# Second experts of a two-attention kernel take token chunks in the order in which attention completes them

## The chip, the core and the metric

The kernel runs on one core of a Trainium2 chip. The metric is the device time of one execution in microseconds (us), as the median of three runs. Beside the runs there is one profiled execution, whose trace every duration below is read from.

## What is computed

A residual stream of 1024 tokens with 512 columns passes four layers. Each normalises its input and adds its output to the stream.

```python
x = x + attn_a(layernorm(x))     # 32 heads of 16 columns, 8 groups of keys and values
x = x + ffn(layernorm(x))        # experts, first time
x = x + attn_b(layernorm(x))     # 32 causal heads of 128 columns, weights as 4-bit integers with scales
x = x + ffn(layernorm(x))        # the same experts, second time

def ffn(x):                      # 8 experts of rank 16, two of them per token
    base   = x @ W_base.T + b_base
    rw, sel = top_k(x @ W_router.T, 2)
    w      = softmax of rw, scattered to the 8 experts
    h      = x @ A[e].T                       # 16 numbers per expert
    return base + 2 * sum over e of w[e] * h[e] @ B[e].T
```

The change concerns the last head of attention b and the second use of the experts.

## The kernel before

**Names.** The stream lies in `x_sb`, four chunks `a` of 256 tokens, each with two halves `h` of 128 tokens. Tile `t` is half `t % 2` of chunk `t // 2`. `xT` holds the normalised stream with columns on partitions. `shared` holds the first experts' weights, and later `yT`, the sum over heads of attention b's output, with columns on partitions. `x_hl` holds the input of attention b split into two parts; after the last projection it takes the experts' weights again.

**Attention b.** For each of 32 heads `n` a loop runs over eight query tiles `t` in the order `TURNS = [0, 6, 1, 7, 2, 4, 3, 5]`. `probabilities` makes the scores (L846), the causal mask (L849), the largest score (L851, VectorE), the exponentials (L855, ScalarE), their sum and the division (L856, L857, VectorE), and moves the result with a DMA from `x_sb` to a `moved` buffer (L860). The stream is out of the way during attention b: it was stored in the DRAM tensor `x_kept` (L941), and the four chunks of `x_sb` serve as slots for probabilities, by the count of tiles modulo 4 (L852). Three tiles later (`LAG = 3`), `behind` turns the probabilities on TensorE (`transposed`, L878, copied by ScalarE at L879).

**Sets.** A head's tiles form two sets of chunks, `SETS = (0, 3), (1, 2)`. When all four tiles of a set are turned, `context` multiplies them with the values (L888), splits the result into a high part (L900, ScalarE) and a low part (L901, VectorE), and queues `project_out`. That multiplies with the output weights (L782, L783, four pairs of matmuls) and adds to `yT` on VectorE (L923, four instructions). Set 0 of a head is full after tiles 0, 6, 1, 7; set 1 after tiles 2, 4, 3, 5.

**What sets the order.** TensorE's order is the order of the calls in the source, interleaved by two lists: `short` and `long`. `fill` takes a share from a list, `complete` takes one named item to its end, `drain` takes both lists to their end. The orders of the other engines and of the DMA queue of SyncE (SP) are arranged when the program is built; each engine then works strictly in its order. PSUM banks for all of this come from one pool of five (`bank`).

**After the last head.** The source goes on as follows.

```python
while lagging:                       # three tiles left: 4, 3, 5
    behind(0); fill(short, shares[0]); behind(1); fill(long, shares[1])
nc.sync.dma_start(x_sb, x_kept)      # whole stream, one DMA of 2 MB
drain()
...
back(0); back(1); turned(0); back(2); moe.base(0); turned(1); back(3)
moe.route(0, 4); moe.base(1); turned(2); turned(3); moe.route(4, 8); ...
```

`back(a)` turns attention's output back (L1064, eight transposes on TensorE), adds it to the stream (L1065), takes the statistics (L154, L155), the scale (L159 to L161) and writes the normalised rows: half 0 on VectorE (L167), half 1 on ScalarE (L175). Then GpSimd adds the experts' bias to the stream (`bias`, L572). `turned(a)` turns the rows on TensorE (L190), copies them to `xT` alternately by ScalarE (L139) and VectorE (L141), and multiplies with the experts' first weights and the router (`hidden`, L579). `route(t0, t1)` picks two experts for four tiles with some twenty small VectorE instructions (L610 to L635). `base(t)` is the dense part (L591, four matmuls), `moe.turned` turns the weighted hidden numbers (L645), and `finish(t)` adds the experts' part (L652) and the stream (L654, VectorE). The result is stored by chunks (L1097, four DMAs of 512 KB).

Of the kernel before, what the change touches and what calls it, by code (L numbers as in the profile page):

```python
# [11 lines left out]
F32 = mybir.dt.float32  # L12
# [8 lines left out]
P = 128  # L21
S = 1024
C = 512
NC_ = C // P
NT = S // P
# [16 lines left out]
def kernel(  # L42
# [28 lines left out]
    nc = tc.nc  # L71

    def pool(stack, name, bufs=1, space=None):
        kw = {} if space is None else {"space": space}
        return stack.enter_context(tc.tile_pool(name=name, bufs=bufs, **kw))
# [5 lines left out]
    out_v = out.rearrange("(a p h) c -> p a h c", p=P, h=2)  # L81
    x_sb = const.tile([P, 4, 2, C], F32, name="x_sb")
    for a in range(4):
# [13 lines left out]
        fill=-BIG,  # L97
# [19 lines left out]
    AR = E * R + E  # L117
    fw = {}

    def place_ffn_weights(room):  # L120
        at = 0
        for name, n, width in ("base", NC_, C), ("ar", NC_, AR), ("b", 1, C), ("bias", 1, C):
            fw[name] = room[:, at : at + n * width].rearrange("p (c o) -> p c o", o=width)
            at += n * width
        return room[:, :at]
# [10 lines left out]
    def evacuate(dst, src):  # L136
        turn[0] += 1
        if turn[0] % 2:
            nc.scalar.copy(dst, src)  # L139
        else:  # L140
            nc.vector.tensor_copy(dst, src)  # L141

    class Norm:


        def __init__(self):
            self.st = const.tile([P, NT, 6], F32, name="st")
            self.mv = const.tile([P, NT, 2], F32, name="mv")
            self.rstd = const.tile([P, NT], F32, name="rstd")
            self.shift = const.tile([P, NT], F32, name="shift")  # L150
# [411 lines left out]
    class Experts:  # L562


        def __init__(self, name, sb, bank):
            self.name, self.sb, self.bank, self.ys = name, sb, bank, {}
            self.hl = sb.tile([P, NT, E * R + E], F32, name="hl")
            self.hw = sb.tile([P, NT, E, R], F32, name="hw")
            self.hwT = sb.tile([P, S], F32, name="hwT")
# [6 lines left out]
        def hidden(self, t):  # L576
            ph = self.bank()
            for c in range(NC_):
                nc.tensor.matmul(  # L579
                    ph[:, :AR],  # L580
                    xT[:, c, ts(t, P)],
                    fw["ar"][:, c, :],
                    start=(c == 0),
                    stop=(c == NC_ - 1),
                )
            evacuate(self.hl[:, t, :], ph[:, :AR])

        def base(self, t):
            py = self.ys[t] = self.bank()
# [59 lines left out]

        def finish(self, t):  # L650
            py = self.ys.pop(t)
            nc.tensor.matmul(py, self.hwT[:, ts(t, P)], fw["b"][:, 0, :], start=False, stop=True)  # L652
            a, h = t // 2, t % 2
            nc.vector.tensor_tensor(x_sb[:, a, h, :], x_sb[:, a, h, :], py, ALU.add)  # L654


    def attention_b():
# [5 lines left out]
        with ExitStack() as ph:  # L663
# [96 lines left out]
            def fill(lane, ns):  # L760
                credit[id(lane)] += ns
                while lane and credit[id(lane)] > 0:
                    credit[id(lane)] -= advance(lane, lane[0])
                if not lane:
                    credit[id(lane)] = 0

            def drain():
                while short or long:
                    fill(short, 4 * FAST)
                    fill(long, SLOW)  # L770

            def complete(name):
                for lane in (short, long):
                    for item in [q for q in lane if q[0] == name]:
                        while item in lane:
                            advance(lane, item)
# [61 lines left out]
            def probabilities(n, t):  # L838

                qT, kT = qTs[n], kTs[n // J]  # L840
                keys = (t + 1) * P
                wide = t >= NT // 2 or (n == 0 and t == 1)
                sc = sc_ps.tile([P, S if wide else C], F32, tag=f"sc{wide}", name="sc")
                for k0 in range(0, keys, C):
                    k1 = min(k0 + C, keys)
                    nc.tensor.matmul(  # L846
                        sc[:, k0:k1], qT[:, ts(t, P)], kT[:, k0:k1], start=True, stop=(k1 < keys)
                    )
                nc.tensor.matmul(sc[:, ts(t, P)], ident_bf, causal_bf, start=False, stop=True)  # L849
                m = work.tile([P, 1], F32, tag="m", name="m", bufs=3)  # L850
                nc.vector.tensor_reduce(m, sc[:, :keys], AX.X, ALU.max, negate=True)  # L851
                p = x_sb[:, len(issued) % 4].rearrange("p h c -> p (h c)")  # L852
                issued.append(t)
                total = work.tile([P, 1], F32, tag="total", name="total", bufs=3)
                nc.scalar.activation(p[:, :keys], sc[:, :keys], AF.Exp, bias=m, accum_out=total)  # L855
                nc.vector.reciprocal(total, total)  # L856
                nc.vector.tensor_scalar_mul(p[:, :keys], p[:, :keys], total)  # L857

                moved = late[0].tile([P, S if wide else C], F32R, tag=f"moved{wide}", name="moved")
                nc.sync.dma_start(moved[:, :keys].bitcast(F32), p[:, :keys])  # L860
                return moved
# [41 lines left out]
                short.append([("o", n, which), 8 * FAST, project_out(n, which)])  # L903

            HALVES = 4

            def project_out(n, which):

# [24 lines left out]
            with tc.manual_schedule(engines={mybir.EngineType.PE}):  # L933
# [62 lines left out]
                def behind(part):  # L996
                    n, t, p = lagging[0]
                    which = int(t // 2 in SETS[1])
                    if part == 0:
                        complete(("c", n - 1, which))  # L1000
                    if part == 0 or t >= 4:
                        transposed(n, t, p, 4 * part)
                    if part:
                        lagging.pop(0)
                        seen[n, which] = seen.get((n, which), 0) + 1
                        if seen[n, which] == 4:
                            complete(("v", n // J))
                            cost = 18 * P * SLOW // C
                            long.append([("c", n, which), cost, context(n, which)])

                for n in range(HEADS):
# [29 lines left out]
                    complete(("q", n + 1))  # L1041
                    if j == J - 1:
                        complete(("k", g + 1))
                while lagging:
                    behind(0)
                    fill(short, shares[0])
                    behind(1)
                    fill(long, shares[1])
                nc.sync.dma_start(x_sb, x_kept)
                drain()  # L1050
                late.pop()
                last.close()
                sb = pool(ph, "f2_sb")
                moe = Experts("2", sb, bank)
                xns = [sb.tile([P, 2, C], F32, name=f"xn{i}") for i in range(2)]
                weights = place_ffn_weights(x_hl.rearrange("p i c s -> p (i c s)").bitcast(F32))
                nc.sync.dma_start(weights, w_kept)

                def back(a):
                    for h in range(2):  # L1060
                        py = bank()
                        for c in range(NC_):
                            y = yT[:, c, ts(a, 2 * P)].rearrange("q (p h) -> q h p", h=2)
                            nc.tensor.transpose(py[:, ts(c, P)], y[:, h], ident)  # L1064
                        nc.vector.tensor_tensor(x_sb[:, a, h, :], x_sb[:, a, h, :], py, ALU.add)  # L1065
                    norm.stats(a)
                    norm.scale(a, a + 1)
                    norm.rows(a, xns[a % 2])
                    moe.bias(a)

                def turned(a):
                    norm.turned(a, xns[a % 2], bank, False, to_xT)
                    for t in (2 * a, 2 * a + 1):
                        moe.hidden(t)

                back(0)
                back(1)
                turned(0)
                back(2)
                moe.base(0)  # L1080
                turned(1)
                back(3)
                moe.route(0, 4)
                moe.base(1)
                turned(2)
                turned(3)
                moe.route(4, 8)
                moe.base(2)
                moe.turned(0, 4)
                for t in range(NT):  # L1090
                    moe.finish(t)
                    if t + 3 < NT:
                        moe.base(t + 3)
                    if t == 2:
                        moe.turned(4, 8)
                    if t % 2:
                        nc.sync.dma_start(out_v[:, t // 2], x_sb[:, t // 2])  # L1097

    attention_a()
    attention_b()  # L1100
# [69 lines left out]
```

## Time and profile before

| what | value |
| --- | --- |
| median of 3 runs | 1600.74 us (1598.55 to 1603.12) |
| the profiled execution's own time | 1601.31 us |
| its span, first to last instruction | 1599.5 us |
| TensorE (PE) busy | 1531.5 us, 96% of the span |
| VectorE (DVE) busy | 1241.1 us, 78% |
| ScalarE (ACT) busy | 783.0 us, 49% |
| GpSimd (POOL) busy | 482.6 us, 30% |
| mean granted TensorE clock | 0.987 of full speed |
| last score of the last head | 1512.5 us |
| start of the first `back` on TensorE | 1529.9 us |
| last matmul | 1595.1 us |

The page of the profile gives busy time by engine and, in 40 slices, where it lies. The timeline lists an engine's instructions in order, with the idle time in front of each in brackets and what ended it. The chain of waits follows the work that ended last backwards. The rows of windows give, for a stretch, the busy time of PE, PEld (weight load), DVE, ACT and POOL, then the granted clock, the share of the DMA engines and GB/s.

### The profile page before, as it was taken

To read this page: it belongs to the slowest core of one execution; us is meant where nothing else is said; L and a number is where in the kernel's file an instruction comes from. 1 tells how busy PE (TensorE), PEld (TensorE's weight loads), DVE (VectorE), ACT (ScalarE), POOL (GpSimd) and SP (SyncE) were. 2 spreads that over 40 slices of the span, in tenths; PEclk is the share of its full clock that TensorE was granted. 3 is DMA by queue.
4 is the path that set the end of the run, shared out by engine and by line. 5 is a ranking of instruction groups with operands and counts; after the bars stand their busy time and mean duration, and the time that the engine had idled before them with its cause. 6 is when DMAs were issued, how large, how long until landed. Compare 5 with 4: busy or idle time off the path is not lost.

```text
span 1599.5 us, 24080 instructions
## 1 busy us (share of the span) xinstructions
PE 1531.5 (96%) x8119; PEld 990.9 (62%) x8119; DVE 1241.1 (78%) x2290; ACT 783.0 (49%) x1694; POOL 482.6 (30%) x382
## 2 busy tenths in 40 slices
PE   7899999999999989999999999999999999999978
PEld 4244444444445457777777777777777777777764
DVE  4689888799755686788888878888788788788763
ACT  2067666576673245544544544444444444454420
POOL 5200000000103154436336336335435335333120
PEclk9899999999999989999999999999999999999999
DMA  5432322324304133333334334333333334333311
GB/s 126 81 81 47 54 49 48 66 36 88 91 3 110 66 105 125 108 139 124 116 131 139 112 119 135 116 119 126 120 120 121 109 120 129 105 112 129 140 50 53
DMA packets 98010, 158.63 MB, mean 99 GB/s; under 512 B 14320, under 2 KB 53936, under 8 KB 97504
## 3 DMA queue, kind: packets, MB, share of 16 engines
q1 hardware_dynamic: 97024, 155.46, 32.6%
q0 software_dynamic: 864, 1.64, 0.7%
q8 instruction: 65, 1.06, 0.3%
q14 instruction: 57, 0.47, 0.1%
HBM read 33.03 MB, written 6.05 MB: 24 GB/s over the span
## 4 chain that ended last, share of the span: by engine, by line
PE 80%; DVE 12%; ACT 3%; issue 2%; DMA 2%; SPq 1%; POOL 0%; ACTq 0%; DVEq 0%; POOLq 0%
PE pc L888 16%; PE sc L846 15%; PE po L413 7%; PE sc L339 6%; PE pp L782 5%; DVE m L348 5%; PE pp L783 5%; PE tp L878 5%; PE py L782 3%; PE py L783 3%; PE bank L591 3%; PE pp L273 2%; PE st L380 2%; PE py L453 2%; PE st L388 2%
## 5 line engine op out<-in xcount | busy, mean ns | idle before, releaser
L348 DVE TENSOR_REDUCE m<-sc 128x1 f32<-128x512 f32 x512 | 320.7, 681 | 37.3 <-PE st L380 21.7
L855 ACT ACTIVATE x_sb<-sc,m 128x768 f32<-128x768 f32 (+7 forms) x256 | 189.7, 741 | 317.1 <-DVE m L851 311.2
L392 ACT ACTIVATE pT<-st 128x512 f32<-128x512 f32 x512 | 264.7, 603 | 125.6 <-PE st L388 111.7
L846 PE MATMUL sc<-kT,qT 128*128 128x512 f32 (+3 forms) x768 | 293.1, 491 | 4.5 <-ACT x_sb L855 2.9
L851 DVE TENSOR_REDUCE m<-sc 128x1 f32<-128x768 f32 (+7 forms) x256 | 192.7, 753 | 132.5 <-PE sc L849 130.9
L888 PE MATMUL pc<-xT,v_sb 128*128 128x256 f32 (+1 forms) x1024 | 248.5, 373 | 5.0 <-DVE acc L796 2.5
L339 PE MATMUL sc<-ks,qs 64*128 64x512 f32 x512 | 187.0, 455 | 9.8 <-DMA ks<-k_hl 4.5
L857 DVE TENSOR_SCALAR x_sb<-x_sb,total 128x768 f32<-128x768 f32 (+7 forms) x256 | 190.0, 743 | 4.6 <-DVE total L856 0.3
L888 PEld LDWEIGHTS pc<-xT,v_sb 128*128 128x128 f32 x1024 | 176.0, 190 | 21.8 <-DVE acc L796 3.2
L846 PEld LDWEIGHTS sc<-kT,qT 128*128 128x128 f32 x768 | 139.6, 193 | 74.8 <-issue 63.8
L339 PEld LDWEIGHTS sc<-ks,qs 64*128 64x128 f32 x512 | 83.5, 186 | 158.5 <-DVE m L348 128.1
L380 PE MATMUL st<-qs,ks 64*128 64x512 f32 x512 | 177.4, 425 | 2.9 <-ACT pT L392 1.7
L388 PE MATMUL st<-ms_q,ones 64*128 64x512 f32 x512 | 179.0, 414 | 0.3 <-DMA ms_q<-mT 0.3
L923 DVE SCALAR_TENSOR_TENSOR shared<-py,o_sc,shared 128x512 f32<-128x512 f32 x248 | 176.1, 739 | 3.8 <-PE py L783 3.7
L808 POOL TENSOR_TENSOR qT<-acc,cos_sb 128x512 f32<-128x512 f32 x62 | 81.7, 1318 | 298.6 <-DVE total L856 203.1
L782 PE MATMUL pp<-x_hl,w 128*128 128x512 f32 x384 | 167.4, 436 | 1.9 <-DVE acc L796 1.3
L879 ACT COPY xT<-tp 128x512 f32<-128x512 f32 (+2 forms) x320 | 137.2, 471 | 63.9 <-PE tp L878 63.6
L783 PE MATMUL pp<-x_hl,w 128*128 128x512 f32 x384 | 152.7, 398 | 2.4 <-DVE x_hl L740 2.4
L690 POOL TENSOR_SCALAR w<-r 128x512 fp32r<-128x512 int32 x80 | 123.5, 1544 | 102.9 <-PE pp L783 69.8
L796 DVE SCALAR_TENSOR_TENSOR acc<-pp,q_sc,acc 128x512 f32<-128x512 f32 x192 | 142.9, 745 | 13.4 <-ACT acc L794 7.0
L878 PEld LDWEIGHTS tp<-ident_r,moved 128*128 128x128 f32 x1152 | 125.3, 141 | 37.0 <-issue 2.2
L413 PE MATMUL po<-pT,v_sb 128*32 128x512 f32 x1024 | 137.5, 608 | 0.0
(169 smaller groups left out, 2176.4 us busy)
## 6 DMA issues: line engine op xcount, KB each, us to landing
turned<-acc SPq DMA_DIRECT2D x160, 128.0 KB
moved<-x_sb SPq DMA_DIRECT2D x32, 512.0 KB
moved<-x_sb SPq DMA_DIRECT2D x32, 448.0 KB
moved<-x_sb SPq DMA_DIRECT2D x32, 384.0 KB
moved<-x_sb SPq DMA_DIRECT2D x32, 320.0 KB
qs<-shared SPq DMA_DIRECT2D x128, 64.0 KB
r<-in_qwq_dram SPq DMA_DIRECT2D x32, 256.0 KB
r<-in_qwo_dram SPq DMA_DIRECT2D x32, 256.0 KB
```

Of the source, the lines that this page charges most:

```text
L339: nc.tensor.matmul(sc, qs[pair % NS][rows, jj, ts(t, P)], ks[pair // 2 % NS][rows, ts(half, C)], start=True, stop=True,)
L348: nc.vector.tensor_reduce(ms[pair][:, at : at + 1], sc, AX.X, ALU.max, negate=True)
L380: nc.tensor.matmul(st, ks[pair // 2 % NS][rows, ts(kt, P)], qs[pair % NS][rows, u // 2, ts(u % 2, C)], start=True, stop=False,)
L388: nc.tensor.matmul(st, ones[rows], ms_q[pair % 2][rows, u // 2, ts(u % 2, C)], start=False, stop=True)
L392: nc.scalar.activation(pTs[pair, kt][:, u], st, AF.Exp, scale=DA**-0.5)
L413: nc.tensor.matmul(po[ts(u, 32), :], v_sb[:, kt, pair // 2, :], pT[:, u], start=(kt == 0), stop=(kt == NT - 1),)
L782: nc.tensor.matmul(ps, lhsT, high, start=True, stop=False)
L783: nc.tensor.matmul(ps, lhsT, low, start=False, stop=True)
L846: nc.tensor.matmul(sc[:, k0:k1], qT[:, ts(t, P)], kT[:, k0:k1], start=True, stop=(k1 < keys))
L851: nc.vector.tensor_reduce(m, sc[:, :keys], AX.X, ALU.max, negate=True)
L878: nc.tensor.transpose(tp[:, k - k0, :].bitcast(F32R), p[:, ts(k, P)], ident_r)
L888: nc.tensor.matmul(pc[:, 2 * P * i + lo : 2 * P * (i + 1)], v_sb[:, k, ts(g, DB)], place[pair][:, k, lo:], start=(k == 0), stop=(k == 2 * ...
```

## The change

1. In the last head, the slot of a tile's probabilities is taken from `SLOTS = 0, 1, 2, 3, 0, 3, 1, 2`: tile 4 goes to slot 3 (before: 1), tile 3 to slot 1 (before: 2), tile 5 to slot 2 (before: 3).
2. The stream comes back by chunks, in four DMAs of 512 KB, chunks 0 and 3 ahead of the last three tiles' turning in the source, chunks 1 and 2 behind it.
3. After the last head's loop, `project_out` of the head before and the last head's first context (chunks 0 and 3) are taken to their end; the first `project_out` follows after the turning of tile 4, `back(0)` after that of tile 3, and `back(3)` after that of tile 5.
4. The normalised rows of all four chunks have a place of their own, in columns 0 to 511 of `v_sb` (values of groups 0 to 3); before, two buffers were used in turn.
5. The second experts take the chunks in the order 0, 3, 1, 2, and tiles in the order 0, 1, 6, 7, 2, 3, 4, 5. Routing, `base` and `finish` follow that order; the biases are added after all four `back`.
6. The result is stored by tiles, in eight DMAs of 256 KB.

```diff
+            self.at = {t: i for i, t in enumerate(tiles)}
-            evacuate(self.hl[:, t, :], ph[:, :AR])
+            evacuate(self.hl[:, self.at[t], :], ph[:, :AR])
...
-                p = x_sb[:, len(issued) % 4].rearrange("p h c -> p (h c)")
+                at = len(issued) - NT * (HEADS - 1)
+                p = x_sb[:, SLOTS[at] if at >= 0 else len(issued) % 4].rearrange("p h c -> p (h c)")
...
-                while lagging:
-                    behind(0)
-                    fill(short, shares[0])
-                    behind(1)
-                    fill(long, shares[1])
-                nc.sync.dma_start(x_sb, x_kept)
-                drain()
...
-                xns = [sb.tile([P, 2, C], F32, name=f"xn{i}") for i in range(2)]
-                weights = place_ffn_weights(x_hl.rearrange("p i c s -> p (i c s)").bitcast(F32))
-                nc.sync.dma_start(weights, w_kept)
+                xns = {
+                    a: v_sb[:, 2 * i : 2 * i + 2, :C] for i, a in enumerate((0, 3, 1, 2))
+                }
...
-                    norm.rows(a, xns[a % 2])
-                    moe.bias(a)
+                    norm.rows(a, xns[a])
...
+                for a in SETS[0]:
+                    nc.sync.dma_start(x_sb[:, a], x_kept[:, a])
+                weights = place_ffn_weights(x_hl.rearrange("p i c s -> p (i c s)").bitcast(F32))
+                nc.sync.dma_start(weights, w_kept)
...
+                complete(("o", HEADS - 2, 1))
+                complete(("c", HEADS - 1, 0))
+                while lagging:
+                    behind(0)
+                    behind(1)
+                    if len(lagging) == 2:
+                        complete(("o", HEADS - 1, 0))
+                    else:
+                        back(SETS[0][1 - len(lagging)])
+                drain()
+                for a in SETS[1]:
+                    nc.sync.dma_start(x_sb[:, a], x_kept[:, a])
...
+                moe = Experts("2", sb, bank, (0, 1, 6, 7, 2, 3, 4, 5))
-                back(0)
+                turned(0)
                 back(1)
-                turned(0)
+                turned(3)
                 back(2)
+                for a in (0, 3, 1, 2):
+                    moe.bias(a)
+                moe.route(0, 4)
                 moe.base(0)
+                moe.base(1)
                 turned(1)
-                back(3)
-                moe.route(0, 4)
-                moe.base(1)
                 turned(2)
-                turned(3)
+                moe.turned(0, 4)
                 moe.route(4, 8)
-                moe.base(2)
-                moe.turned(0, 4)
-                for t in range(NT):
+                todo = list(moe.at)
+                moe.base(6)
+                for i, t in enumerate(todo):
                     moe.finish(t)
-                    if t + 3 < NT:
-                        moe.base(t + 3)
-                    if t == 2:
+                    if i + 3 < NT:
+                        moe.base(todo[i + 3])
+                    if i == 2:
                         moe.turned(4, 8)
-                    if t % 2:
-                        nc.sync.dma_start(out_v[:, t // 2], x_sb[:, t // 2])
+                    nc.sync.dma_start(out_v[:, t // 2, t % 2], x_sb[:, t // 2, t % 2])
```

## The prediction, made before the changed kernel had run

> **What bounds the kernel now.** I read the page first. Rows are in tenths of 40 slices.
>
> ```profile
> PE   7899999999999989999999999999999999999978
> ...
> PEclk9899999999999989999999999999999999999999
> ```
>
> TensorE (PE) is full nearly everywhere, so what the change can win lies where PE is not full: the last two slices. The orders of instructions of both built programs agree on every engine up to tile 7 of the last head, so nothing before about 1507 us moves. I then read PE's timeline from the last score (1512.5) to the end; the bracket is idle time.
>
> ```profile
> 1529.93 2.45 PE L1064 MATMUL bank<-ident,shared 128*128 128x128 f32 x16
> 1537.23 2.30 PE L190 MATMUL bank<-ident,xn 128*128 128x128 f32 x8 [4.85 <-DVE rstd L160]
> ...
> 1559.60 1.84 PE L579 MATMUL bank<-x_hl,xT 128*128 128x136 f32 x12 [2.02 <-DVE xT L141]
> ...
> 1592.32 2.74 PE L652 MATMUL bank<-x_hl,hwT 128*128 128x512 f32 x6
> ```
>
> The large hole is 4.85 us in front of the first turning of normalised rows. The chain of waits (start, us, what) says what fills it:
>
> ```profile
> 1530.72 0.74 DVE shared L923
> 1531.46 1.19 DVE x_sb L1065 x2
> 1532.65 0.67 DVE st L154 x2
> ...
> 1536.91 0.82 ACT xn L175
> 1537.78 1.75 PE bank L190 x7
> 1539.53 3.87 PE bank L579 x16
> ...
> 1595.10 0.69 DVE x_sb L654
> ```
>
> Two chunks' sums, statistics and rows on VectorE take 1531.46 to 1537.8, 6.35 us, with PE out of work. Last, the granted clock (third number from the right) in stretches of 3 us:
>
> ```profile
> 1537.00:1540.00 3.00, 2.67 (x11) 2.18 (x12) 1.21 (x5) 2.01 (x3) 2.19 (x1) 0.51 0.00 0
> 1540.00:1543.00 3.00, 3.00 (x15) 2.99 (x15) 0.26 (x1) 0.27 (x1) 2.47 (x2) 0.50 0.02 5
> ...
> 1558.00:1561.00 3.00, 1.40 (x11) 1.41 (x12) 2.64 (x12) 0.57 (x3) 0.67 (x1) 0.99 0.00 0
> 1561.00:1564.00 3.00, 3.00 (x15) 2.77 (x14) 1.78 (x4) 0.58 (x1) 0.00 (x0) 0.50 0.00 0
> ```
>
> Behind each of the two holes PE runs at half clock: by rows of 1 us from 1537.0 to 1543.8 and from 1561.0 to 1564.3. Half of the time is lost there: (6.6 + 3.4) / 2 = 5.0 us.
>
> **The account of before**, from 1512.7 (behind the last score) to the span's end at 1599.5, 86.8 us: PE idle 0.68 (probabilities of tile 5), 0.67 + 0.23 (context's parts), 4.85, 0.24 + 0.24 (copies to xT), 2.02, 0.67 (hwT), together 9.6; half clock 5.0; from the last matmul (1595.1) to the end 4.4; the rest, 67.7, is PE's work with some 1.4 of small gaps, and the change leaves its instructions as they are.
>
> **The change part by part.** I followed PE's new order with before's durations: a pair of L782 and L783 0.47, context 0.43 per full matmul (3.84 a set), eight transposes of `back` 0.95, of `turned` 1.04, `hidden` for two tiles 2.15, `base` 3.43, `finish` 0.86; L923 0.68 apart, L900 0.6, L901 0.65.
>
> *Slots.* Tile 4 takes the slot of tile 7, only two tiles back, whose move is out at 1508.6 (rows of 1 us: 385 GB/s, then 164). Its exponential began at 1508.24 and now also stands behind a context copy (0.6): 0.9 later. Its move lands at 1513.4, and PE turns it at 1518.4. Nothing, with 5 us of cover; beyond that us for us.
>
> *Restores, on SP's queue.* Order now: move 2, chunk 0, moves 4 and 3, chunks 3 and 1, move 5, chunk 2. Each restore waits for a landing and holds the moves behind it. The old 2 MB went out at 1518.45 and flowed until 1525; half a MB flows in some 1.5 us after 1 us of start. Chunk 0: issued 1508.9, in by 1511.8. Chunk 3: issued 1513.4 (move 4), in by 1516.3. Chunk 1: issued 1514.8 (move 3). Move 5 is ready at 1516.85 (1 us later than before, since two L923 stand ahead of its scaling), lands at 1519.6, is needed at 1523.8. Nothing, with 4 us of cover.
>
> *PE after the last score.* Four pairs for head 30 to 1516.05, the rest of context (31, 0) to 1518.6, turning of tile 4. The project_out of (31, 0) waits for L900 (idle 0.5) and L901 (0.4), ends 1521.5; tile 3; `back(0)` waits for its last L923 at 1523.1 (idle 0.9); tile 5; `back(3)` to 1525.1; context (31, 1), 3.84, to 1528.95. This hides VectorE's 6.35 us, now 1523.35 to 1529.7: the 4.85 hole is gone.
>
> *The wait that comes instead.* In ScalarE's new order the high part of context (31, 1) stands behind the rows of chunks 0 and 3. They end 6.97 us after VectorE begins (1531.46 to 1538.43 before): 1530.35. The copy is done at 1530.95 where context was ready at 1529.1; the low part at 1531.6. PE idles 2.05 + 0.4. Queued behind on PE: all the rest.
>
> *Second experts.* Turned(0) from 1533.3: idle 0.5, as the VectorE copy follows four L923. Turned(3): its VectorE copy now stands behind `back(1)`'s sums and statistics, 1.3. (Before, a `base` covered that.) Two `base`, 6.9 us, cover the rows of chunk 2 and most of route(0, 4), which ends at 1552.0 against PE's 1550.05; turned(1)'s VectorE copy comes behind it: 0.95. Turned(2): 0.2. Turning of hw: hidden behind the sixth `base`, which takes away before's 0.67. Idle in sum: 0.9 + 0.9 + 2.45 + 0.5 + 1.3 + 0.95 + 0.2 = 7.2.
>
> *Stores.* The last one moves 256 KB instead of 512. Before, the last two flowed at some 400 GB/s in 1595 to 1598; half of the last one's 1.4 us goes, 0.6. Four more issues of 0.33 each lie on an idle SP; if it were not idle, 1.3.
>
> *Weights, rows in v_sb, tile mapping, order of biases on GpSimd:* nothing. The weights' DMA moves in the source only: on SP it stands where it stood, issued at 1476. Groups 0 to 3 were last read by head 15; the mapping only changes addresses; a bias starts when its chunk's rows are written, and is read by L654 20 us later. Without that cover each costs its 2.35.
>
> [...] The row:
>
> ```profile
> 1556.59 2.12 DVE L611 TENSOR_TENSOR eq<-rest,m 128x32 f32<-128x32 f32 x1
> ...
> 1556.33 2.34 POOL L572 TENSOR_TENSOR x_sb<-x_sb,x_hl 128x1024 f32<-128x1024 f32 x1 [5.39 <-ACT xn L175]
> ```
>
> Elsewhere such an L611 takes 0.19; here it ends with the bias. [...] Now routing of the first four tiles meets the biases of chunk 1 (from 1542.6) and chunk 2 (from 1547.2). With one meeting, as in before, the 0.95 stands (without it 0, so a gain is possible); if both meet, 1.9 more. [...] I take one meeting.
>
> **A rule and the clock.** The trace went to half clock after 2.02 us of idle within 3.4 us, for 3.4 us; after 4.85 for 6.8. [...] By the trace one period of half clock follows, 3.4 / 2 = 1.7. [...]
>
> **Sum.** 67.7 work + 7.2 idle + 1.7 clock + 3.8 end = 80.4 against 86.8: 6.4 less. The profiled run's own 1601.31 (span 1599.5 and 1.8 around it) becomes 1594.9; it is 0.6 above the median, so the median 1600.74 becomes 1594.3. A measurement of this kernel can tell about 0.3%, 4.8 us, from no change.
>
> **The rivals.**
>
> *The clock eats it (0.18).* [...]
>
> *ScalarE's queue holds context (31, 1) far longer (0.08), slower.* The copy behind both chunks' rows has no cover: each us is a us of PE. The rows need chunk 3 from `x_kept`, needed at 1525.9 (second sum on VectorE), due at 1516.3. It decides from a landing 9.6 + 6.4 + 4.8 us late, at about 1537: then 1605.5 and above. Against it: the whole 2 MB took 7 us in before.
>
> *The early chunks are not early.* The built orders exclude it: on PE both `back` stand ahead of context (31, 1).
>
> **How the numbers follow.** My account has 0.74 and gives 1592.6 to 1597.6 with the clock's ends, a us or two lower if the small gaps of before's interleaving (some 1.4 between 1512 and 1530) go too; within it a win above 4.8 needs at most 3.3 lost to clock and ports, which I give 0.87: 0.65 faster, 0.09 same. With the clock rival, same is 0.28; slower 0.07. The range takes in more than half of the clock rival at the top and the bottom of my account: 1590.6 to 1600.6.
>
> **What would show it.** Right: no hole above 3 us on PE after 1512; the first L190 about 4 us earlier, near 1533; a hole of about 2 us in front of the last L782, ended by ScalarE's L900; last matmul near 1589 (1512.7 + 76.6); one 2 us routing instruction. Wrong: PE waiting for `moved` DMAs of tiles 4 or 5; half clock for over two periods; `turned(3)` waiting over 2 us; a span that ends over 4.4 us after the last matmul.

## The result, and the profile after

The kernel after has a median of 1590.84 us over 6 runs (1588.00 to 1594.71). On the same chip the kernel before has 1600.19 us over 6 runs. The medians are 9.35 us apart. The ratio of the runs is 0.9946, with a 95% interval of 0.9927 to 0.9964: between 5.8 and 11.7 us less. The profiled execution of after took 1588.0 us, with a span of 1586.2 us and a mean clock of 0.993 (before: 1601.31, 1599.5 and 0.987).

In the kernel after, most lines of the tail stand one to four lines lower: project_out L783 and L784, context L890 and its copies L902 and L903, the addition to `yT` L927, `hidden` L580, `finish` L653. `back` is L1059 and L1060. In the page of the profile, the same two rows as before:

```profile
PE   7899999999999989999999999999999999999988
...
PEclk9899999999999999999999999999999999999999
```

The last slices are 8 and 8 where they were 7 and 8, and the low clock in slice 15 is gone. That slice lies 900 us ahead of the change, so its clock is not the change's doing. PE's timeline from the turning of chunk 3 to the end:

```profile
1520.13 1.19 PE L1059 MATMUL bank<-ident,shared 128*128 128x128 f32 x8
...
1526.85 0.51 PE L783 MATMUL py<-ctx,w 128*128 128x512 f32 x1 [1.63 <-ACT ctx L902]
1527.58 0.50 PE L784 MATMUL py<-ctx,w 128*128 128x512 f32 x1 [0.22 <-DVE ctx L903]
...
1529.32 1.03 PE L190 MATMUL bank<-ident,v_sb 128*128 128x128 f32 x8
...
1536.85 1.66 PE L580 MATMUL bank<-x_hl,xT 128*128 128x136 f32 x12 [0.91 <-DVE xT L141]
...
1549.03 1.66 PE L580 MATMUL bank<-x_hl,xT 128*128 128x136 f32 x12 [0.87 <-DVE xT L141]
...
1579.61 2.74 PE L653 MATMUL bank<-x_hl,hwT 128*128 128x512 f32 x6
```

The first L190 follows the last project_out without a hole; before, 4.85 us of idle time stood in front of it. The longest hole is now 1.63 us (with 0.22 behind it), in front of the project_out of the last context, and it ends with ScalarE's copy L902. Below it is called the hold. The chain of waits shows what that copy stood behind:

```profile
1519.38 1.29 DVE x_sb L1060 x2
...
1524.83 1.50 ACT v_sb L175 x2
1526.33 0.48 ACT ctx L902
...
1526.83 0.70 DVE ctx L903
```

VectorE's sums and statistics begin at 1519.38 and ScalarE's two rows end at 1526.33, 6.95 us later. PE works on until 1525.2, where the last context ends, so some 5.8 of these us now lie beside its work; the other 1.1 and the copy's 0.48 are the hold. The windows of 3 us at the hold (last numbers: clock, DMA share, GB/s):

```profile
1525.00:1528.00 3.00, 1.15 (x5) 0.59 (x5) 1.48 (x5) 1.80 (x3) 2.29 (x1) 1.00 0.00 0
1528.00:1531.00 3.00, 2.71 (x18) 2.15 (x17) 2.88 (x5) 0.59 (x1) 2.42 (x2) 1.00 0.00 0
```

The clock stays full, although PE is busy for only 1.15 us of the first window.

**The tail.** From the start of the last causal-mask matmul of the last head to the span's end: 86.99 us before (from 1512.52), 78.12 after (from 1508.10). The table splits it for every kernel of this study, from one profiled execution each. "Idle" is the sum of PE's idle times above 0.12 us, "end" is what follows the last matmul, "rest" is what is left. "Half clock" is how long the clock was at half in the tail up to the last matmul, from narrow windows.

| kernel | tail | idle | end | rest | half clock |
| --- | --- | --- | --- | --- | --- |
| before | 86.99 | 9.60 | 4.45 | 72.9 | 10.24 |
| before, with filler (e5) | 83.50 | 6.04, filler 4.3 | 4.44 | 68.7 | 0 |
| after | 78.12 | 5.62 | 3.87 | 68.6 | 0 |
| after again (e0) | 79.35 | 5.57 | 3.88 | 69.9 | 3.41 |
| after again (e9) | 78.12 | 5.63 | 3.88 | 68.6 | 0 |
| no overlap (e1) | 82.98 | 9.38 | 3.88 | 69.7 | 3.41 |
| slots by count (e2) | 79.33 | 5.46 | 3.88 | 70.0 | 3.41 |
| store by chunks (e3) | 80.23 | 5.66 | 4.76 | 69.8 | 3.41 |
| copy between rows (e4) | 77.40 | 4.92 | 3.88 | 68.6 | 0 |
| biases behind routing (e6) | 77.06 | 4.88 | 3.88 | 68.3 | 0 |
| other order (e7) | 79.04 | 5.03 | 3.87 | 70.1 | 3.41 |
| combined (e8) | 75.80 | 3.35 | 3.88 | 68.6 | 0 |

Without half clock the rest is 68.3 to 68.7 us in every kernel: the same work. One period of 3.41 us adds 1.1 to 1.5, and before's 10.24 us, three periods, added 4.3. So the tail's gain of 8.9 us is 4.0 of idle time, 0.6 at the end and 4.3 of half clock: about half of it is the clock. This execution of after had no period; e0's had one, and there the gain is 7.6, with 3.0 of clock. The two profiled executions differ by 13.3 us. The other 4.4 lie ahead of the last score, where both kernels have the same order: there before had 30.7 us of half clock and after 20.5. Other executions of after's tail had 23.9 and 27.3 there, and other changed kernels from 17.1 to 34.1, so this difference is not the change's.

### The profile page after: what moved, and what is told of

It is laid out like the page before. It is cut to its first block, busy times and chain, and to the rows that moved or that the text cites. A ratio compares the mean times of both kernels' runs of the same rounds, so it can differ in the third digit from the quotient of the medians.

```text
span 1586.2 us, 24089 instructions
## 1 busy us (share of the span) xinstructions
PE 1523.3 (96%) x8119; PEld 983.7 (62%) x8119; DVE 1240.0 (78%) x2290; ACT 783.4 (49%) x1694; POOL 482.5 (30%) x382
## 4 chain that ended last, share of the span: by engine, by line
PE 80%; DVE 12%; ACT 3%; issue 2%; DMA 2%; SPq 1%; POOL 0%; ACTq 0%; DVEq 0%; POOLq 0%
PE pc L890 16%; PE sc L847 15%; PE po L413 7%; PE sc L339 6%; PE pp L783 5%; PE pp L784 5%; DVE m L348 5%; PE tp L880 5%; PE py L783 4%; PE py L784 3%; PE bank L592 3%; PE pp L273 2%; PE st L380 2%; PE py L453 2%; PE st L388 2%
## 5 line engine op out<-in xcount | busy, mean ns | idle before, releaser
L890 PE MATMUL pc<-xT,v_sb 128*128 128x256 f32 (+1 forms) x1024 | 247.6, 373 | 5.6 <-DVE shared L927 2.5
L890 PEld LDWEIGHTS pc<-xT,v_sb 128*128 128x128 f32 x1024 | 175.6, 189 | 22.8 <-DVE shared L927 3.3
L927 DVE SCALAR_TENSOR_TENSOR shared<-py,o_sc,shared 128x512 f32<-128x512 f32 x248 | 175.8, 738 | 1.8 <-PE py L784 1.7
L783 PE MATMUL pp<-x_hl,w 128*128 128x512 f32 x384 | 166.4, 433 | 1.9 <-DVE acc L797 1.3
L784 PE MATMUL pp<-x_hl,w 128*128 128x512 f32 x384 | 151.9, 396 | 2.4 <-DVE x_hl L741 2.4
```

Source lines behind the costliest of these rows:

```text
L783: nc.tensor.matmul(ps, lhsT, high, start=True, stop=False)
L784: nc.tensor.matmul(ps, lhsT, low, start=False, stop=True)
L890: nc.tensor.matmul(pc[:, 2 * P * i + lo : 2 * P * (i + 1)], v_sb[:, k, ts(g, DB)], place[pair][:, k, lo:], start=(k == 0), stop=(k == 2 * ...
```

## The experiments

Theory A is the prediction's: what counts is that VectorE's work for two `back` lies beside the last context, and what is then lost is the hold at ScalarE's copy. Rivals are that the DMAs' side (slots, restores, stores) brings the gain, and that the gain is the clock's alone. Runs of before in the same comparisons had medians of 1599.61 (e1, e2, e3, e5), 1599.09 (e0, e4, e6, e7) and 1599.39 us (e8, e9).

**e1: everything but the overlap.** Both `back` go behind the last context and its project_out.

```diff
                     if len(lagging) == 2:
                         complete(("o", HEADS - 1, 0))
-                    else:
-                        back(SETS[0][1 - len(lagging)])
                 drain()
+                back(0)
+                back(3)
```

> The changed kernel with back(0) and back(3) put behind the last drain, so that no VectorE work of theirs lies beside the last context; all else stays. I count the tail, from the start of the last causal-mask matmul to the span's end: 87.0 us before, 78.1 us after. Theory A (the win is the 6.35 us of VectorE work hidden behind the last context, and the half clock that the hole brought): the hole of some 4.9 us in front of the first L190 is back, the hold in front of the last project_out shrinks from 1.85 to 0.9, so the tail is 82 us, and 85 with the half clock behind the hole: 4 to 7 us slower than the changed kernel. Theory B (the win is on the DMA side: early restores, slots, smaller stores): the tail stays within 1 us of 78.1.

Measured: 1597.29 us (20 runs), 0.9984 of before (0.9974 to 0.9994), and 6.5 us above after's median. PE's timeline:

```profile
1531.79 2.07 PE L1059 MATMUL bank<-ident,shared 128*128 128x128 f32 x16
1539.08 2.20 PE L190 MATMUL bank<-ident,v_sb 128*128 128x128 f32 x8 [5.22 <-DVE rstd L160]
```

The hole is back, 5.22 us behind the sixteen transposes, and with it a period of half clock. The tail is 4.9 us longer than after's, 82.98 where 85 was expected with half clock: the period cost 1.1. PE's idle time is 9.38 us, nearly before's 9.60, so without the overlap hardly any of the 4.0 us is won. The overlap carries the larger part of the gain. What is left of it against before is 1.0 to 4.2 us for the slots, the restores, the stores and the order of tiles together.

**e2: the slots of before.** The last head takes slots by the count again.

```diff
-                p = x_sb[:, SLOTS[at] if at >= 0 else len(issued) % 4]...
+                p = x_sb[:, len(issued) % 4]...
```

> The changed kernel with the slots of the last head taken by the count modulo 4, as before (tile 4 in slot 1, tile 3 in slot 2, tile 5 in slot 3). Chunk 3's restore then waits for move 5 instead of move 4, some 2.5 us later. Theory A: chunk 3 is needed only at the second sum on VectorE, 7 us after it would land, so the tail stays at 78.1 within 0.5. Theory B: the restore is late and chunk 3's rows hold the last context; the tail is 2 us or more longer.

Measured: 1590.64 us (6 runs), 0.9952 (0.9936 to 0.9967). SP's queue (the move of tile 5, then chunk 3's restore, which in after went out at 1509.86):

```profile
1513.77 0.47 SPq L862 DMA_DIRECT2D moved<-x_sb  x1
1518.23 0.32 SPq L1071 DMA_DIRECT2D x_sb<-x_kept  x1
```

Chunk 3's restore now waits for the move of tile 5, and nothing on PE waits for it. The hold is 1.63 us, as in after. The tail is 1.2 us longer than expected by theory A, and the same as that of e0 (79.33 and 79.35), which also has one period of half clock. The slots are worth nothing in this order.

**e3: the stores of before.** Four stores of 512 KB.

```diff
-                    nc.sync.dma_start(out_v[:, t // 2, t % 2], x_sb[:, t // 2, t % 2])
+                    if t % 2:
+                        nc.sync.dma_start(out_v[:, t // 2], x_sb[:, t // 2])
```

> The changed kernel with four stores of 512 KB instead of eight of 256 KB, each behind its chunk's second tile. Theory A: only the last store counts, its flow grows from 0.8 to 1.4 us, tail 78.7 (+0.6). Theory B: stores carry several us, tail over 80.

Measured: 1593.15 us (11 runs), 0.9959 (0.9941 to 0.9976). In the profile 4.76 us follow the last matmul where after has 3.87: stores by tiles are worth 0.9 us there. The tail of 80.23 is over the 80 of theory B, but it holds one period of half clock; e0 and e2, which hold one too, have 79.3, so 0.9 is left for the stores. The median can't separate that from after.

**e5: before, with its large hole filled.** Ten matmuls whose result nobody reads, behind the second `back` (five calls, which make ten matmuls in the trace), so that PE isn't idle while VectorE works; all else is before's.

```diff
                 back(0)
                 back(1)
+                warm = bank()
+                for i in range(5):
+                    nc.tensor.matmul(warm, ident, cos_sb[:, :C], start=(i == 0), stop=(i == 4))
```

> The kernel before with five more matmuls of 128x512 (a constant, into a PSUM bank that nothing reads, 4.3 us) put on TensorE in the 4.85 us hole between back(1) and turned(0). They do no useful work. If the half clock behind the hole is caused by the hole and costs what I counted (3.3 of the 5.0 us): no half clock from the hole on, tail 83.7 instead of 87.0, although the work has grown. If the clock falls for another reason, or if the half clock costs nothing because something else holds the pace: tail 87 or longer.

Measured: 1598.48 us (12 runs), 0.9996 (0.9982 to 1.0009). PE's timeline:

```profile
1530.25 4.46 PE L1080 MATMUL bank<-cos_sb,ident 128*128 128x512 f32 x10
1535.27 0.30 PE L190 MATMUL bank<-ident,xn 128*128 128x128 f32 x1 [0.56 <-DVE rstd L160]
```

The hole of 4.85 us became 4.3 us of filler and 0.56 of idle time. In the tail no half clock is left, and it is 3.5 us shorter than before's, with 0.7 us more of filler and idle time. So before's half clock, three periods, cost 4.2 us in that execution. Only the two behind the large hole went with the filler. The third followed a hole of 2.02 us in front of L579; e5 still has that hole (1553.2 to 1555.2), at full clock (last section). That the gain doesn't show in the median (interval −2.9 to +1.4 us) is explained only in part: by mean clock and span (below) e5 loses 3.1 us less to the clock than before, and 1.6 more elsewhere, of which the filler and idle time explain 0.7; the other 0.9 stays open. Keeping the clock here, without the overlap, does not give the gain of this change.

**e0 and e9: after itself, again,** as controls of the later comparisons.

> The changed kernel itself, on the chip of the next three, to compare them with. Holes on TensorE as in its first profile (1.63 in front of the last project_out, 0.91 and 0.87 in hidden). If a hole of 1.6 us brings half clock in some executions only, by where it falls in a window, its times spread by the clock alone: time less the clock's loss should agree within 1 us between executions.

> The changed kernel itself, on the chip of the combined version, to compare it with. Tail 78.1 without and 79.4 with half clock behind the hole of 1.63 + 0.22, by whether both parts fall in one window of the clock.

Measured: 1589.56 us (5 runs), 0.9941 (0.9929 to 0.9953), and 1592.94 (8 runs), 0.9954 (0.9938 to 0.997). The profile of e0 shows another execution of the same hold, windows as above:

```profile
1525.00:1528.00 3.00, 1.15 (x6) 0.61 (x4) 1.80 (x5) 2.12 (x4) 1.97 (x1) 1.00 0.00 0
1528.00:1531.00 3.00, 3.00 (x9) 2.26 (x10) 2.31 (x4) 0.00 (x0) 2.72 (x2) 0.56 0.00 0
```

The instructions and the hold are the same (1.15 us busy in the first window), but the second window has a clock of 0.56, and the tail is 1.2 us longer. Of the six executions that have this hold unchanged (after, e0, e2, e3, e6, e9), three had the half clock behind it and three had not. One expectation failed: time less the clock's loss does not agree within 1 us. In e0 it is 1574.0 to 1575.3 in four runs and 1580.7 in the fifth, for which there is no trace; its cause stays open.

**e4: the copy between the rows.** The rows of chunks 0 and 3 are written in the source behind the last context; in the built order ScalarE's copy then stands between its two rows.

```diff
                     norm.scale(a, a + 1)
-                    norm.rows(a, xns[a])
+                    if a not in SETS[0]:
+                        norm.rows(a, xns[a])
...
                 drain()
+                for a in SETS[0]:
+                    norm.rows(a, xns[a])
```

> The changed kernel with the rows of chunks 0 and 3 written behind drain in the source, which moves one instruction: on ScalarE the high copy of context (31, 1) now stands between the two rows instead of behind both. If the hold is ScalarE's order, as the prediction said, the copy starts at the end of the first row, 0.65 us earlier: the hole of 1.63 in front of the last project_out becomes about 1.0 and the tail falls from 78.1 to 77.5. If the hold is the low part on VectorE, or the context itself, the hole only moves to the second matmul and the tail stays.

Measured: 1590.92 us (5 runs), 0.995 (0.9937 to 0.9963). ScalarE's timeline:

```profile
1527.16 0.80 ACT L175 ACTIVATE v_sb<-x_sb,shift,rstd 128x512 f32<-128x512 f32 x1
1527.87 0.56 ACT L902 CAST ctx<-pc 128x512 fp32r<-128x512 f32 x1
1528.33 0.81 ACT L175 ACTIVATE v_sb<-x_sb,shift,rstd 128x512 f32<-128x512 f32 x1
```

With one row less ahead of the copy, PE's hold shrinks from 1.63 to 0.93 us and the tail by 0.7. The median doesn't show it (e0 has 1589.56 in the same comparison). So the hold is set by ScalarE's order, and its size by what stands ahead of the copy.

**e6: two biases behind the routing.** The biases of chunks 1 and 2 are read from a copy in `cos_sb` that is finished only when `route(0, 4)` is (a VectorE instruction that reads the routing's last output writes its first element).

```diff
-                for a in (0, 3, 1, 2):
+                for a in (0, 3):
                     moe.bias(a)
                 moe.route(0, 4)
+                bias = cos_sb[:, :C].rearrange("p (i o) -> p i o", i=1)
+                nc.gpsimd.tensor_copy(bias, fw["bias"])
+                nc.vector.tensor_scalar(
+                    bias[:, 0, :1], moe.hw[:, 3, E - 1, R - 1 :], 0.0, fw["bias"][:, 0, :1], ALU.mult, ALU.add
+                )
+                for a in (1, 2):
+                    moe.bias(a, bias)
```

> The changed kernel with GpSimd's biases of chunks 1 and 2 made to wait for the first routing's result (they read a copy of the bias in a dead table, one element of which VectorE rewrites behind the routing), so that no bias runs beside routing. [...] If GpSimd has no part in it, the 2 us instruction stays 2 us, and the tail 78.1.

Measured: 1590.19 us (5 runs), 0.9948 (0.9936 to 0.996). First the timelines of VectorE and GpSimd in after, then VectorE's and PE's in e6 (whose lines are one lower):

```profile
1543.77 2.06 DVE L612 TENSOR_TENSOR eq<-rest,m 128x32 f32<-128x32 f32 x1
...
1543.44 2.34 POOL L573 TENSOR_TENSOR x_sb<-x_sb,x_hl 128x1024 f32<-128x1024 f32 x1 [2.40 <-ACT v_sb L175]
```

```profile
1544.57 0.19 DVE L613 TENSOR_TENSOR eq<-rest,m 128x32 f32<-128x32 f32 x1
```

The routing instruction that takes 2.06 us in after and ends with the bias (1545.83 and 1545.78) takes 0.19 us where no bias runs beside it. PE's wait of 0.87 in front of L580 at 1549 is gone:

```profile
1548.24 2.20 PE L581 MATMUL bank<-x_hl,xT 128*128 128x136 f32 x16 [0.24 <-ACT xT L139]
```

The tail is 1.1 us shorter, 77.06 for after's 78.12. The median doesn't show it (e0 again 1589.56).

**e7: an order without the known holes.** `back(3)` behind the last context, a `base` between the two `turned`, the next two `base` ahead of `turned(1)`, `moe.turned(0, 4)` ahead of `turned(2)`, the biases of e6. The diff shows the first part.

```diff
-                    else:
-                        back(SETS[0][1 - len(lagging)])
+                    elif len(lagging) == 1:
+                        back(0)
+                complete(("c", HEADS - 1, 1))
+                back(3)
                 drain()
...
                 turned(0)
-                back(1)
+                moe.base(0)
                 turned(3)
+                back(1)
                 back(2)
```

> A version built from what the profile after shows: back(3) stands between the last context and its project_out (so that PE has 1 us of work while ScalarE copies the context), base(0) directly behind turned(0), turned(3) ahead of back(1), base(1) and base(6) ahead of turned(1), and the biases behind routing as in the run before. If the four holes 1.85, 0.91, 0.87 and the short ones are what is left to win, the tail falls by 2.5 to 3, to 75 to 75.6 without half clock, and with no hole over 1 us the clock does not fall in it: some 1587 in the median. If VectorE is the bound of the tail, holes come back elsewhere and the tail stays at 77 to 78.

Measured: 1590.58 us (6 runs), 0.995 (0.9937 to 0.9964): no gain over after. PE's and VectorE's timelines:

```profile
1537.60 2.24 PE L581 MATMUL bank<-x_hl,xT 128*128 128x136 f32 x12 [2.09 <-DVE xT L141]
...
1536.20 0.74 DVE L928 SCALAR_TENSOR_TENSOR shared<-py,o_sc,shared 128x512 f32<-128x512 f32 x1
1536.86 0.68 DVE L141 COPY xT<-bank 128x512 f32<-128x512 f32 x1
```

The hold at ScalarE's copy is gone (PE waits 0.67 us for the low part on VectorE), and a hole of 2.09 us stands in `hidden` of chunk 0 instead, with half clock behind it. The tail is 79.04, some 77.5 without the period: not the 75 to 75.6 of the first case, but the 77 to 78 of the second, in which VectorE is the bound. Its copy L141 on VectorE now stands behind chunk 3's sums and statistics and the additions of the last project_out (L928). The edit moved the wait from ScalarE's queue to VectorE's.

**e8: e4 and e6, and a `base` between the turning of chunk 3 and its `hidden`.**

```diff
-                turned(3)
+                turned(3, (0,))      # transposes, base(0), then hidden
...
+                moe.base(6)          # before: behind moe.turned(0, 4)
                 turned(1)
```

> The changed kernel with the three single gains together, VectorE's order around the last context left as it was (the run that put back(3) beside it had only moved the hole): the high copy between the rows, the biases of chunks 1 and 2 behind routing, base(0) between turned(3)'s transposes and its hidden, base(1) and base(6) ahead of turned(1). By the account: holes 1.63 to 0.93, 0.91 and 0.87 to none, tail 78.1 - 0.7 - 0.9 - 0.9 = 75.6 us; no window of 3.4 us holds 1.7 us of idle PE, so no half clock in the tail in any execution. Median 2 to 3 us below the changed kernel's. If VectorE is the bound, a new hole of 1 us or more stands in front of hidden or of the last project_out, and the tail stays above 77.

Measured: 1590.16 us (6 runs), 0.994 (0.9921 to 0.9959); after in the same comparison (e9) has 0.9954. PE's timeline:

```profile
1534.93 0.51 PE L784 MATMUL py<-ctx,w 128*128 128x512 f32 x1 [0.93 <-ACT ctx L903]
...
1546.32 2.02 PE L581 MATMUL bank<-x_hl,xT 128*128 128x136 f32 x16
...
1564.07 1.12 PE L654 MATMUL bank<-x_hl,hwT 128*128 128x512 f32 x2 [0.68 <-ACT hwT L139]
```

The hold is 0.93, chunk 3's `hidden` no longer waits, and a wait of 0.68 for hwT is new. The tail is the shortest of all, 75.80 us for an expected 75.6, 2.3 below after's, and without half clock. The 1.7 us of idle time in the expectation was an estimate; the last section has what windows of 3.41 us showed. The medians put e8 2.8 us below e9, with overlapping intervals; but e9 is the highest of after's three medians, and the others are 1590.84 and 1589.56. It is the best version by the trace, and not shown to be faster in time.

**Taking the clock out.** The loss to the clock is taken as (1 − mean clock) times the span; since the clock is given to 0.001, it comes in steps of 1.6 us for a single run. Over the 63 runs of before in the later comparisons the mean time is 1599.6 us, the loss 19.4, the difference 1580.3. Over the 19 runs of after (with e0 and e9) these are 1591.2, 14.8 and 1576.4. So the gain of 8.5 us is 4.6 of clock and 3.9 of the rest. The 20 runs of e1 have 1597.4, 18.0 and 1579.5 (rounded apart): against after they lose 3.1 us to the clock and 3.1 in the rest, which is most of the 3.9. The standard deviation of after's 19 times is 2.5 us, and of the times less the loss 1.7: the clock is a good part of the spread from run to run, and not all of it.

## Why the prediction was right, and where it was off

Predicted were 6.4 us of gain and a time of 1594.3, in a range of 1590.6 to 1600.6; measured were 9.35 and 1590.84. The direction and the main step were right, the size was too small. The time lies only 0.2 us above the lower end of the range, and the same kernel's five runs in e0 have a median below it, 1589.56: that it fell inside was in part luck. In the tail 6.4 were predicted and 8.9 measured; 1.6 of the missing 2.5 us is idle time and 1.0 the clock (rounded apart).

- **The hidden 6.35 us (right).** The 4.85 hole is gone; e1 brings it back, and 6.5 us of the time with it. With before's times (4.42 us later) the first L190 is at 1533.7 for a predicted 1533.3, and the last matmul ends at 1586.8 for "near 1589".
- **The new hold at ScalarE's copy (right, too large).** Predicted 2.05 + 0.4, measured 1.63 + 0.22. The rows' end was costed well (6.95 us from VectorE's beginning for 6.97). With before's times the context ended at 1529.63 for a predicted 1528.95, 0.7 later, and ScalarE's copy at 1531.23 for 1530.95, only 0.3 later; so the hole was 0.4 shorter. For the low part 0.4 was put, where before's own rows have 0.23. e4 shows that ScalarE's order is the cause.
- **The other idle times.** Context (31, 0) 0.9 predicted, 0.55 measured; `back(0)` 0.9, 0.42; turned(0) 0.5, 0.29; turned(3) 1.3, 1.15; turned(1) 0.95, 1.11; turned(2) 0.2, 0.24. Together 7.2 were predicted and 5.6 measured: this term of the sum was 1.6 too high, most of it in the hold (0.6), in `back(0)` (0.5), whose first transposes ran while the additions were still under way, and in context (31, 0) (0.35).
- **The clock (mis-sized twice).** Before's 5.0 was taken as half of the time at half clock (6.6, not 6.8, since PE starts at 1537.23). By e5 and by the rest column it was 4.2 to 4.3: matmuls took less than twice as long at half clock (last section). After's 1.7 stood in the sum in full; its ends (1592.6 and 1597.6) put the loss at 0 and 5. It cost 1.2 (e0 against after) and came in three executions of six, and no run shows the end of 5. So the clock's term was a gain of 3.3 in the prediction, and is 4.3 in the profiled pair and 4.6 in the means.
- **Stores (right).** Predicted 0.6; the end is 4.45 before and 3.87 after, and e3 gives 0.9.
- **Slots (right: nothing), by e2.** Restores: no wait on PE for a DMA in the tail; chunk 3's was issued at 1509.86, with before's times 1514.3 for a predicted 1513.4. Whether four restores instead of one matter was not run alone; e1 bounds everything beside the overlap to 1.0 to 4.2 us.
- **The routing instruction beside a bias (right, in part by luck).** One meeting was taken, and one instruction of 2.06 us came (L612 at 1543.77, beside the bias of 1543.44 to 1545.78). The other bias, of chunk 1, ended at 1541.04, 0.5 us before the routing's first L612 (1541.54). e6 prices the meeting at 1.1 us for a predicted 0.95. Not every VectorE instruction was slowed: in after two sums (L1060 at 1539.06, 1.28 us together) ran beside a bias in their usual time, and so did the routing's first maximum (L611 at 1538.95, 0.18). The odds speak of ports: no run shows a port as the cause, only the 1.87 us by which the instruction was longer (2.06 for 0.19) and e6's 1.1.
- **The small gaps of before's interleaving (not seen).** Without half clock the rest is 68.7 us in before (e5) and 68.6 in after; the us or two that the prediction held possible there did not come.
- **The rivals.** The clock did not eat the gain: in three profiled executions never more than one period in after's tail. ScalarE's hold never waited for a restore.

The rule that the prediction read off the trace, one period after 2.02 us of idle time, did not hold as put: in e5 the same 2.02 us in front of the same line brought none, and after's hold of 1.63 + 0.22 brought one in three of its six executions. In before and after half clock followed windows of 3.41 us in which PE was idle for 1.69 us or more (last section).

## What to carry to other kernels

Where one engine's serial work (here sums, statistics and rows on VectorE) stands alone between two stages, put it beside the last long stretch of the busy engine; then look which small copy on a third engine now stands in its queue behind that work, since here that was the new hole. When filling such holes one by one, follow every copy's place in its own queue: e7 took one wait away and made another of the same size. Where the time spreads by 0.4% from run to run, compare span and mean clock beside the medians, over many runs; the gain in work can then be told from the gain in clock. A single run can lie 5 us off, as one in e0 does.

## What the runs showed of the hardware that was not expected

- **Half clock after less than 3.41 us of idle time.** Up to the last matmul, half-clock stretches in these traces last 3.41 us or a multiple, and within a trace they start a multiple of 3.41 us apart (before: 1537.04 for 6.83 us and 1560.94 for 3.41 us, seven times 3.41 apart); so one can lay a grid of 3.41 us and sum PE's idle time in each window of it. In the tail, windows at full clock with 1.86, 1.86 and 1.85 us idle (e2, e3, e0), 2.02 and 3.41 (before), 2.09 (e7) and 3.36 (e1) were followed by half clock; 1.63 (after, e9), 1.25 (e6), 1.14 (e4) and 1.44 (e5) were not. In e0, e2 and e3 both parts of the hold, 1.63 and 0.22, fall into one window, in after into two. In e5 the hole of 2.02 is split, and the fuller window is the one with 1.44. Outside the tail, in before and after from 42 us on, no window at full clock with 1.44 us idle or less was followed by half clock, and those with 1.69 (before, 417.47 to 420.88) or more were, but for one of 1.84 (after, 550.87 to 554.28); in e1's tail one of 1.86 was not either. An estimate from these windows puts the limit near half of 3.41 us; an exact rule was not shown.
- **The grid has no fixed place against the kernel.** Around the hold (PE busy for 1.15 us from 1525 to 1528 in both) after has a border of its grid at 1527.08, and e0 near 1528.4, where its half clock begins (0.56 from 1528 to 1531). The same hold cost a period in three executions of six. That the 17 to 34 us of half clock ahead of the tail differ between executions for the same reason was argued, not shown.
- **A period costs less than half of itself.** 3.41 us at half clock cost 1.1 to 1.5 us in the tail, 1.2 between two executions of the same kernel, and not 1.7. The same sixteen matmuls in before, at half clock and at full, show one reason:

```profile
1539.35 4.05 PE L579 MATMUL bank<-x_hl,xT 128*128 128x136 f32 x16
...
1549.15 2.20 PE L579 MATMUL bank<-x_hl,xT 128*128 128x136 f32 x16 [0.24 <-ACT xT L139]
```

They take 1.84 times as long, not twice. The second line also shows a wait of 0.24 us for a copy that the slower work does not have.
